# Attention scores split between GpSimd and VectorE: half of the squares of 16, a later row sum and an earlier fold

## The chip, the cores and the metric

The kernel runs on one core of a Trainium2 chip, as one program. The metric is the device time of one execution in microseconds (us). The engines are TensorE (PE in the profile; PEld is its weight load), VectorE (DVE), ScalarE (ACT), GpSimd (POOL) and SyncE (SP). POOL and SP issue the DMAs of this kernel.

## What is computed

A block of a small network over x of 8 batches x 512 tokens x 256 features, fp32: attention A, FFN, attention B, FFN again, each on the layer norm of x and added to it. The change touches attention A alone. It is an odd attention: for each token and each of its 16 heads, the 64 channels of Q attend to the 64 channels of K of the same token.

```python
Q = (x @ Wq + bq).reshape(b, s, H, C) * inv_sqrt_c      # H = 16, C = 64
K = (x @ Wk + bk).reshape(b, s, H, C)
V = (x @ Wv + bv).reshape(b, s, H, C)
scores = jnp.einsum('bshq,bshk->bshqk', Q, K)
mask = jnp.triu(jnp.ones((C, C), dtype=bool), 1)
scores = jnp.where(mask, -jnp.inf, scores)
w = jax.nn.softmax(scores, axis=-1)
attn = jnp.einsum('bshqk,bshk->bshq', w, V)
```

So every token and head has a 64 x 64 lower triangle of products q_i * k_j, their exponentials, and two row sums: of the exponentials, and of the exponentials times v_j. Nothing of this is a matmul; it is elementwise work on DVE, ACT and POOL.

## The kernel before

Tokens lie on the 128 partitions. A cell is one batch b (8), one group g of four heads (4) and one tile i of 128 tokens (4): 128 cells. The triangle of a cell is cut into the diagonal, and squares of 32, 16, 8, 4, 2 and 1 below it. They make four units (`units`, `NU`): unit 0 has the squares of 32 of two heads, unit 1 the squares of 16 of all four, unit 2 the squares of 32 of the other two heads, unit 3 all small squares. Each unit holds two halves in one tile, the exponentials e and the products e*v. Units 0 and 2 share the tag "w" with three buffers; unit 1 has the tag "w16" and unit 3 the tag "ws", with one buffer each.

A unit goes through these stages, each a method of `AttentionA`:

- `scores` (L765; the multiply is L784): q_i * k_j into the first half, two pieces of 128x1024 for the units 0 to 2. Before the change the units 0 and 2 are on POOL, which reads q from a copy in SBUF, and the units 1 and 3 on DVE.
- `exps` (L789; L798): exponential on ACT.
- `weigh` (L800; L808): e * v_j on DVE.
- `halve` (L810; L814): an accumulating DMA of 1 MB, issued by POOL, adds the second half of the columns of the tile to the first half (units 0 to 2).
- `fold` (L816; L819): for the units 0 and 2, POOL adds halves once more, 2048 columns to 1024.
- `gather` (L838; L845): row sums on DVE into small tiles `red`; the tile of the unit is free after it. The pairs (n, red) are put on the list `self.sums`.
- `add_rows` (L848; L852): POOL adds the sums to the cell's `acc`, which starts with the diagonal. `small_squares` (L828) does the same for the squares of 2 and 1, with L835.
- `invert` (L854; L856): reciprocal of the sum of exponentials on DVE; `divide` (L858; L860): the product on POOL.

Before `scores`, `project` computes q, k, v with PE, and `keep_qk` copies k and q to SBUF with ACT. After `divide`, `turn_group`, `project_out` and `new_x` bring the result back to x.

All engines but SP follow an order written out by hand: instructions stand on each engine in the order in which the Python program emits them. The order is `step(n)` (L638), a software pipeline over all 512 units: step n emits the scores of unit n, the weighing and halving DMA of unit n - 2, the fold of a unit n - 3 or n - 4, and so on. A step has three parts, split by `yield`. Between the parts the loop at the end of the file emits pieces of the generator `after_a` (FFN, attention B and FFN of batches whose attention A is done), at a rate set by `total`. So the first 75 steps have attention A alone with preparation, and the end has the last batch's FFN alone.

The generator `later_weights` (L411) prepares weights of the later stages on POOL, ACT and SP, and bounds on the inputs. `fit_qkv(g)` subtracts a row from the weights of head group g (group 0 on DVE, the others on POOL) and stores them to DRAM for later loads by `load_w` on SP. `measure(b)` (L726) makes mean and variance of x for the layer norm of a batch.

Of the kernel before, what the change touches and what calls it, by code (L numbers as in the profile page):

```python
# [9 lines left out]
F32 = mybir.dt.float32  # L10
# [3 lines left out]
ALU = mybir.AluOpType  # L14
AX = mybir.AxisListType

P = 128
# [9 lines left out]
GW = GH * C  # L27
NG = HID // GW
# [256 lines left out]
def fast_path(ctx: ExitStack, tc: tile.TileContext, k, t, flag):  # L285

    nc = tc.nc
# [8 lines left out]
    ap_ = ctx.enter_context(tc.tile_pool(name="ap", bufs=2))  # L296
# [257 lines left out]
    NU = len(units)  # L554
# [12 lines left out]
    def pieces(w, n, off, nsq, cols):  # L567

        def of_rows(v):
            return v[:, cols].rearrange("p (x t) -> p x t", t=2 * n)[:, :, n:]

        def of_cols(v):
            return v[:, cols].rearrange("p (x t) -> p x t", t=2 * n)[:, :, :n]

        if n < 16:
            e, ev = (  # L580
                w[:, a * SMALL + off : a * SMALL + off + nsq * n * n].rearrange("p (x i j) -> p x i j", i=n, j=n)
                for a in range(2)
            )
            yield e, ev, lambda v: of_rows(v).unsqueeze(3), lambda v: of_cols(v).unsqueeze(2)
            return
        both = w.rearrange("p (b a x i j) -> p a b x i j", a=2, x=nsq, i=n, j=JB)
        if n == 32:
            for x in range(nsq):
                yield (
                    both[:, 0, :, x],  # L590
                    both[:, 1, :, x],
                    lambda v, x=x: of_rows(v)[:, x].unsqueeze(1).unsqueeze(3),
                    lambda v, x=x: of_cols(v)[:, x].rearrange("p (b j) -> p b j", j=JB).unsqueeze(2),
                )
        else:
            for k in range(n // JB):
                yield (
                    both[:, 0, k],
                    both[:, 1, k],
                    lambda v: of_rows(v).unsqueeze(3),  # L600
                    lambda v, k=k: of_cols(v)[:, :, k * JB : (k + 1) * JB].unsqueeze(2),
                )

    class AttentionA:
# [32 lines left out]

        def step(self, n):  # L638

            weighed = self.at(n - 2)  # L640
            if weighed[0] is not None:
                self.weigh(*weighed)
            unit = self.at(n)
            on_pool = unit[3] in (0, 2)
            if on_pool:
                half = self.scores(*unit)
                next(half)
            if weighed[0] is not None:
                self.halve(*weighed)
            if on_pool:  # L650
                next(half, None)
            b, i, g, u = self.at(n + 40)
            if u == 0 and g == 0 and i == 0 and b > 0:
                self.x[b] = load_x(b)
            b, i, g, u = self.at(n + 10)
            if u == 0 and g == 0 and i == 0:
                self.measure(b)
            b, i, g, u = self.at(n + 8)
            if u == 0 and g == 0:
                self.live["xn"] = normed(self.x[b][:, i, :], *self.rn[b, i], "a")  # L660
            b, i, g, u = self.at(n - 5)
            if u == NU - 1:
                self.invert(b, i, g)
            b, i, g, u = self.at(n - 4)
            if u == 1:
                self.gather(b, i, g, u)
            b, i, g, u = self.at(n + 7)
            if u == 0 and g == 0:
                nc.scalar.copy(self.live[b, i], self.live.pop("ps_ln"))
            if self.at(n - 1)[0] is not None:  # L670
                self.exps(*self.at(n - 1))
            yield
            if unit[0] is not None and not on_pool:
                for _ in self.scores(*unit):
                    pass
            for args in self.sums:
                self.add_rows(*args)
            self.sums = []
            b, i, g, u = self.at(n - 5)
            if u == NU - 1:  # L680
                self.divide(b, i, g)
            b, i, g, u = self.at(n - 2)
            if u == NU - 1:
                self.small_squares(b, i, g)

            b, i, g, u = self.at(n - 4)
            if u == 0:
                self.fold(b, i, g, u)
            b, i, g, u = self.at(n - 3)
            if u == 2:  # L690
                self.fold(b, i, g, u)
            b, i, g, u = self.at(n - 9)
            if u == NU - 1:
                self.new_x(b, i, g)
            b, i, g, u = self.at(n + 2)
            if u == 0:
                self.keep_qk(b, i, g)
            b, i, g, u = self.at(n - 7)
            if u == NU - 1:
                self.turn_group(b, i, g)  # L700
            b, i, g, u = self.at(n - 8)
            if u == NU - 1:
                self.project_out(b, i, g)
            b, i, g, u = self.at(n + 3)
            if u == 0:
                self.project(b, i, g)
            yield
            b, i, g, u = self.at(n - 4)
            if u == 2:
                self.gather(b, i, g, u)  # L710
            b, i, g, u = self.at(n - 5)
            if u == 0:
                self.gather(b, i, g, u)
            b, i, g, u = self.at(n - 3)
            if u == NU - 1:
                self.gather(b, i, g, u)
            b, i, g, u = self.at(n - 7)
            if u == NU - 1:
                nc.scalar.copy(self.live["att"], self.live.pop("pta"))
            b, i, g, u = self.at(n + 8)  # L720
            if u == 0 and g == 0:
                self.live[b, i] = lnp.tile([P, DC, P], F32, tag="xnt_a", name=f"xnta_{b}_{i}", bufs=NT)
                self.live["ps_ln"] = turned_over(self.live.pop("xn"), half_bank().rearrange("p (c s) -> p c s", c=DC))
            yield
# [40 lines left out]
        def scores(self, b, i, g, n_u):  # L765

            qv, kt = self.live[b, i, g][:2]
            if n_u == 0:
                acc = ap_.tile([P, 2, GW], F32, tag="acc", name=f"acc_{b}_{i}_{g}", bufs=3)
                self.live[b, i, g].append(acc)  # L770
                nc.vector.tensor_tensor(acc[:, 0, :], qv[:, 0], kt[:, 0], ALU.mult)

            if n_u in (0, 2):
                w = wt.tile([P, 4096], F32, tag="w", name=f"w_{b}_{i}_{g}_{n_u}", bufs=3)
            elif n_u == 1:
                w = wt.tile([P, 4096], F32, tag="w16", name=f"w16_{b}_{i}_{g}")
            else:
                w = wt.tile([P, 2 * SMALL], F32, tag="ws", name=f"ws_{b}_{i}_{g}")
            self.live[b, i, g, n_u] = w
            eng, q = (nc.gpsimd, kt[:, 1]) if n_u in (0, 2) else (nc.vector, qv[:, 0])  # L780
            for n, off, nsq, cols in squares(units[n_u]):
                for e, ev, rows, columns in pieces(w, n, off, nsq, cols):
                    shape = list(e.shape)
                    eng.tensor_tensor(  # L784
                        e, rows(q).to_broadcast(shape), columns(kt[:, 0]).to_broadcast(shape), ALU.mult
                    )
                    yield
# [50 lines left out]
        def gather(self, b, i, g, n_u):  # L838


            w = self.live.pop((b, i, g, n_u))
            for n, off, nsq, cols in squares(units[n_u]):
                if n > 2:
                    red = ap_.tile([P, 2, nsq * n], F32, tag=f"red{nsq * n}", name=f"red_{b}_{i}_{g}_{n_u}_{n}", bufs=2 + (n < 32))
                    nc.vector.tensor_reduce(red, self.columns_of(w, n, off, nsq), AX.X, ALU.add)  # L845
                    self.sums.append((b, i, g, n, cols, red))

        def add_rows(self, b, i, g, n, cols, part):  # L848

# [491 lines left out]
    with tc.manual_schedule(engines={ET.PE, ET.DVE, ET.Activation, ET.Pool}):  # L1341
        a = AttentionA()
        prep = later_weights()
        fit_qkv(0)
        weights = None
        done, spent = after_a(), 0
        for n in range(-10, a.steps):
            for part, _ in enumerate(a.step(n)):
                if n >= 2:
                    next(prep, None)  # L1350
                while 3 * spent * each < total * (3 * (n - each - 11) + part + 1):
                    spent += next(done)
            if 0 <= n < NG - 1:
                fit_qkv(n + 1)
        for _ in done:
            pass
    judge()
# [86 lines left out]
```

## Time and profile before

| what | us |
|---|---|
| median of 3 runs | 4010.42 (4006.96 to 4017.54) |
| time of the profiled execution | 4009.55 |
| its span | 4007.6 |
| L784 on POOL (scores of 32), 512 | 1076.2 busy, 2102 ns each |
| L784 on DVE, 128x1024 of the squares of 16, 256 | 301.3 busy, 1219 ns each |
| L819 on POOL (fold), 256 | 643.1 busy, 2512 ns each |
| L814 on POOL (halving DMA issue), 384 | 337.1 busy, 878 ns each |
| L852 on POOL, row sums of 32 (128x128), 256 | 179.4 busy, 701 ns each |
| L852 on POOL, other row sums of a `red` (128x256), 384 | 291.6 busy, 759 ns each |
| L845 on DVE, row sums of 16 (128x256 out of 128x2048), 128 | 292.0 busy, 2281 ns each |
| L845 on DVE, row sums of 32 (128x128 out of 128x1024), 256 | 309.7 busy, 1210 ns each |
| L856 on DVE (reciprocal), 128 | 223.2 busy, 1744 ns each |

A line of the profile names the source line, the engine, the operation and the tiles (out<-in), the shape, a count, the busy time and the mean duration of one. In a timeline the first column is the start and the second the duration, both in us, and the bracket says how long the engine stood idle before the instruction and what ended that. Neighbours overlap a little on an engine, so the distance from start to start is shorter than the duration. Work of one engine lies beside that of the others, so busy times don't add up to the span.

### The profile page before, as it was taken

The numbers are of one execution on the slowest core, as the hardware profiler recorded it, in microseconds if no ns is written. First come the engines' busy times: TensorE is split into PE (matmuls) and PEld (weight loads), VectorE is DVE, ScalarE is ACT, GpSimd is POOL, SyncE is SP. The second block draws the span as 40 slices with busy tenths as digits, with TensorE's granted clock in tenths as the row PEclk, the third lists the DMA queues.
The fourth block names the chain that finished last, engine by engine and source line by source line (L and its number), as shares of the span: only waits on it lengthen the run. The fifth ranks groups of instructions, "written<-read, shape, count | busy, mean of one in ns | idle before, by whom it ended". The sixth has DMA issues, their size and how long they took to land.

```text
span 4007.6 us, 37678 instructions
## 1 busy us (share of the span) xinstructions
PE 2958.0 (74%) x12328; PEld 2012.2 (50%) x12328; DVE 3376.7 (84%) x3777; ACT 2337.2 (58%) x3145; POOL 3098.1 (77%) x3051
## 2 busy tenths in 40 slices
PE   1543478777876888768787788768787778768988
PEld 0311145355653656346553566346653556436847
DVE  4899988998889888998989988998889988897115
ACT  2433465666755766666755767567656667555342
POOL 6688888887888887887888888888888878886211
PEclk7555689888987989889897889879898899879999
DMA  8566777668776777668776688668877687767304
GB/s 240 114 141 145 146 182 182 147 161 199 199 162 126 195 188 196 150 147 210 174 192 139 168 198 214 147 131 198 195 181 151 154 199 205 155 133 210 126 29 167
DMA packets 118653, 671.07 MB, mean 167 GB/s; under 512 B 12704, under 2 KB 31915, under 8 KB 43824
## 3 DMA queue, kind: packets, MB, share of 16 engines
q0 software_dynamic: 78336, 570.46, 62.9%
q1 hardware_dynamic: 40112, 98.11, 6.8%
q8 instruction: 100, 1.64, 0.2%
q14 instruction: 105, 0.86, 0.1%
HBM read 255.90 MB, written 9.96 MB: 66 GB/s over the span
## 4 chain that ended last, share of the span: by engine, by line
DVE 38%; PE 16%; POOL 14%; DMA 12%; issue 8%; ACT 8%; POOLq 0%; DVEq 0%; ACTq 0%
DVE red L845 15%; DMA w<-w 12%; DVE w L808 10%; PE ph L1120 5%; ACT w L798 3%; POOL w L819 3%; DVE ws L808 3%; POOL w L784 3%; PE pqkb L1167 3%; DVE ws L784 3%; POOL acc L852 3%; DVE w L784 2%; POOL w L814 2%; DVE acc L856 2%; POOL h L1036 2%
## 5 line engine op out<-in xcount | busy, mean ns | idle before, releaser
L798 ACT ACTIVATE w<-w 128x2048 f32<-128x2048 f32 x384 | 734.2, 1913 | 653.8 <-POOL w L784 440.8
L1120 PE MATMUL ph<-h,hidden 128*128 128x512 f32 x4096 | 1047.9, 412 | 77.4 <-POOL h L1036 45.5
L784 POOL TENSOR_TENSOR w<-k 128x1024 f32<-128x1024 f32 x512 | 1076.2, 2102 | 9.6 <-ACT k L762 9.0
L1120 PEld LDWEIGHTS ph<-h,hidden 128*128 128x128 f32 x4096 | 795.3, 196 | 282.1 <-POOL h L1036 55.9
L808 DVE TENSOR_TENSOR w<-w,qv 128x1024 f32<-128x1024 f32 x768 | 899.8, 1213 | 22.4 <-ACT w L798 22.3
L845 DVE TENSOR_REDUCE red<-w 128x128 f32<-128x1024 f32 (+1 forms) x384 | 601.8, 1567 | 171.6 <-DMA w<-w 94.6
L819 POOL TENSOR_TENSOR w<-w 128x1024 f32<-128x1024 f32 x256 | 643.1, 2512 | 72.5 <-DMA w<-w 71.9
L814 POOL DMA_DIRECT2D w<-w x384 | 337.1, 878 | 339.7 <-issue 134.8
L852 POOL TENSOR_TENSOR acc<-acc,red 128x256 f32<-128x256 f32 (+1 forms) x640 | 471.0, 736 | 152.3 <-DVE red L845 124.5
L845 DVE TENSOR_REDUCE red<-ws 128x256 f32<-128x2048 f32 (+1 forms) x256 | 435.5, 1743 | 0.0
L746 PE MATMUL qv<-wqv,xnta 128*128 128x512 f32 x512 | 299.3, 715 | 89.9 <-DVE ws L808 82.4
L808 DVE TENSOR_TENSOR ws<-ws,qv 128x1024 f32<-128x1024 f32 (+3 forms) x512 | 294.7, 638 | 49.4 <-ACT ws L798 49.4
L1052 PE MATMUL pw<-xnt,gate 128*128 128x512 f32 (+2 forms) x1152 | 298.8, 419 | 24.9 <-ACT silu L1028 18.0
L784 DVE TENSOR_TENSOR w<-qv,k 128x1024 f32<-128x1024 f32 x256 | 301.3, 1219 | 3.6
L784 DVE TENSOR_TENSOR ws<-qv,k 128x1024 f32<-128x1024 f32 (+3 forms) x512 | 299.8, 648 | 0.0
L868 PE MATMUL bank<-ident,acc 128*128 128x128 f32 x256 | 64.3, 341 | 287.5 <-ACT k L761 287.1
L798 ACT ACTIVATE ws<-ws 128x1920 f32<-128x1920 f32 x128 | 231.5, 1809 | 75.3 <-DVE ws L784 74.7
L1052 PEld LDWEIGHTS pw<-xnt,gate 128*128 128x128 f32 x1152 | 227.6, 213 | 82.1 <-ACT silu L1028 22.3
L1229 ACT ACTIVATE eb<-psb 128x256 f32<-128x256 f32 (+3 forms) x512 | 182.2, 443 | 146.6 <-PE psb L1226 146.3
L1146 PE MATMUL pof<-w,h 128*128 128x256 f32 x1024 | 247.9, 396 | 19.4 <-ACT h L1085 19.4
L1085 ACT ACTIVATE h<-ph,s_sb 128x512 fp32r<-128x512 f32 (+1 forms) x256 | 171.1, 688 | 145.9 <-PE ph L1120 144.6
L856 DVE RECIPROCAL acc<-acc 128x256 f32<-128x256 f32 x128 | 223.2, 1744 | 12.3 <-POOL acc L852 12.3
(143 smaller groups left out, 4723.5 us busy)
## 6 DMA issues: line engine op xcount, KB each, us to landing
w<-w POOLq DMA_DIRECT2D x384, 1024.0 KB, 7.7
hidden<-in_h POOLq DMA_DIRECT2D x128, 1024.0 KB, 7.9
gate<-in_w12p POOLq DMA_DIRECT2D x32, 1024.0 KB, 9.0
w<-w_d SPq DMA_DIRECT2D x16, 1024.0 KB, 12.0
wqv<-wqv_d SPq DMA_DIRECT2D x31, 512.0 KB
wo<-in_wo SPq DMA_DIRECT2D x32, 256.0 KB, 7.4
wbqk<-wbqk_d SPq DMA_DIRECT2D x8, 1024.0 KB
w<-in_h SPq DMA_DIRECT2D x8, 1024.0 KB, 7.0
```

Source lines behind the costliest of these rows:

```text
L746: nc.tensor.matmul(qv.rearrange("p j f -> p (j f)"), xnt[:, c, :], wqv[:, c, :], start=(c == 0), stop=(c == DC - 1),)
L784: eng.tensor_tensor(e, rows(q).to_broadcast(shape), columns(kt[:, 0]).to_broadcast(shape), ALU.mult)
L798: nc.scalar.activation(e, e, AF.Exp, scale=C**-0.5)
L808: nc.vector.tensor_tensor(ev, e, columns(qv[:, 1]).to_broadcast(list(e.shape)), ALU.mult)
L814: nc.gpsimd.dma_start(w[:, :2048], w[:, 2048:], accum_op=ALU.add)
L819: nc.gpsimd.tensor_tensor(w[:, :1024], w[:, :1024], w[:, 1024:2048], ALU.add)
L845: nc.vector.tensor_reduce(red, self.columns_of(w, n, off, nsq), AX.X, ALU.add)
L852: nc.gpsimd.tensor_tensor(rows, rows, part.rearrange("p a (x i) -> p a x i", i=n), ALU.add)
L856: nc.vector.reciprocal(acc[:, 0, :], acc[:, 0, :])
L1052: nc.tensor.matmul(pj[:, toks], w[:, m % 4, j, c, :], xs[:, p, c, toks], start=(p == 0 and c == 0), stop=(p == 1 and c == DC - 1),)
L1120: nc.tensor.matmul(pss[j], w[:, j, c, :], h_in(p, c), start=(p == 0 and c == 0), stop=(p == 1 and c == MC - 1),)
L1146: nc.tensor.matmul(po, h(0, c)[:, i * P : (i + 1) * P], w3[:, c, :], start=(c == 0), stop=False)
```

## The change

1. In `scores`, the engine is chosen for each piece: all pieces of the squares of 32, and the first of the two pieces of the squares of 16, go to POOL; the second piece of 16 and the small squares to DVE.
2. `gather` for the units 0 and 2 writes into two halves of one tile, `red` of 32, and only the later of them puts it on the list: one `add_rows` of 128x256 instead of two of 128x128. The row sums of unit 2 come a step later (n - 5, not n - 4), those of unit 0 a step earlier (n - 4, not n - 5).
3. `fold` of unit 0 moves from step n - 4 to n - 3, ahead of the step's scores and halving DMA.
4. `invert` and `divide` come a step later (n - 6, not n - 5). `invert` and the `gather` of unit 1 move to the front of their step, in this order; `divide` comes behind the fold of unit 2.
5. At the start: `measure(0)` comes ahead of `fit_qkv(0)`, the fits of the other groups come at steps 4, 14 and 24 rather than 0, 1 and 2, and the preparation advances once a step from step 3, rather than three times a step from step 2.

```diff
         def step(self, n):
 
+            b, i, g, u = self.at(n - 6)
+            if u == NU - 1:
+                self.invert(b, i, g)
+            b, i, g, u = self.at(n - 4)
+            if u == 1:
+                self.gather(b, i, g, u)
             weighed = self.at(n - 2)
             if weighed[0] is not None:
                 self.weigh(*weighed)
+            b, i, g, u = self.at(n - 3)
+            if u == 0:
+                self.fold(b, i, g, u)
             unit = self.at(n)
...
             b, i, g, u = self.at(n + 10)
             if u == 0 and g == 0 and i == 0:
-                self.measure(b)
+                if b > 0:
+                    self.measure(b)
...
-            b, i, g, u = self.at(n - 5)
-            if u == NU - 1:
-                self.invert(b, i, g)
-            b, i, g, u = self.at(n - 4)
-            if u == 1:
-                self.gather(b, i, g, u)
...
             self.sums = []
-            b, i, g, u = self.at(n - 5)
-            if u == NU - 1:
-                self.divide(b, i, g)
             b, i, g, u = self.at(n - 2)
             if u == NU - 1:
                 self.small_squares(b, i, g)
 
-            b, i, g, u = self.at(n - 4)
-            if u == 0:
-                self.fold(b, i, g, u)
             b, i, g, u = self.at(n - 3)
             if u == 2:
                 self.fold(b, i, g, u)
+            b, i, g, u = self.at(n - 6)
+            if u == NU - 1:
+                self.divide(b, i, g)
...
             b, i, g, u = self.at(n - 4)
-            if u == 2:
+            if u == 0:
                 self.gather(b, i, g, u)
             b, i, g, u = self.at(n - 5)
-            if u == 0:
+            if u == 2:
                 self.gather(b, i, g, u)
...
-            eng, q = (nc.gpsimd, kt[:, 1]) if n_u in (0, 2) else (nc.vector, qv[:, 0])
             for n, off, nsq, cols in squares(units[n_u]):
-                for e, ev, rows, columns in pieces(w, n, off, nsq, cols):
+                for p, (e, ev, rows, columns) in enumerate(pieces(w, n, off, nsq, cols)):
+
+                    on_pool = n == 32 or n == 16 and p == 0
+                    eng, q = (nc.gpsimd, kt[:, 1]) if on_pool else (nc.vector, qv[:, 0])
...
                 if n > 2:
-                    red = ap_.tile([P, 2, nsq * n], F32, tag=f"red{nsq * n}", name=f"red_{b}_{i}_{g}_{n_u}_{n}", bufs=2 + (n < 32))
-                    nc.vector.tensor_reduce(red, self.columns_of(w, n, off, nsq), AX.X, ALU.add)
-                    self.sums.append((b, i, g, n, cols, red))
+                    if n_u != 2:
+                        self.live["red", n] = ap_.tile(
+                            [P, 2, GW // 2], F32, tag=f"red{n // 32}", name=f"red{n}_{b}_{i}_{g}"
+                        )
+                    red = self.live["red", n]
+                    part = red[:, :, cols.start // 2 : cols.stop // 2]
+                    nc.vector.tensor_reduce(part, self.columns_of(w, n, off, nsq), AX.X, ALU.add)
+                    if n_u != 0:
+                        self.sums.append((b, i, g, n, slice(0, GW), red))
...
         prep = later_weights()
+        a.measure(0)
         fit_qkv(0)
         weights = None
         done, spent = after_a(), 0
         for n in range(-10, a.steps):
             for part, _ in enumerate(a.step(n)):
-                if n >= 2:
+                if n >= 3 and part == 2:
                     next(prep, None)
...
-            if 0 <= n < NG - 1:
-                fit_qkv(n + 1)
+            if n in (4, 14, 24):
+                fit_qkv(n // 10 + 1)
```

## The prediction

> **What bounds the kernel now.** I read the page's busy shares first, then a table of windows over a stretch where only attention A runs, then the timelines of GpSimd (POOL) and VectorE (DVE) in one period of that stretch, and last the view of the halving DMA's line.
>
> ```profile
> PE 2958.0 (74%) x12328; PEld 2012.2 (50%) x12328; DVE 3376.7 (84%) x3777; ACT 2337.2 (58%) x3145; POOL 3098.1 (77%) x3051
> ```
>
> No engine is full on average, so the stages must be looked at apart. A "cell" below is one (batch, token tile, head group): four steps, 128 cells in all. From 161 to 327 us seven cells run with little beside them:
>
> ```profile
> 208.00:232.00 24.00, 9.41 (x16) 4.49 (x16) 23.97 (x25) 9.12 (x9) 20.72 (x18) 0.57 0.79 176
> sum 166.00, PE 66.78 PEld 31.04 DVE 165.76 ACT 63.86 POOL 145.12; mean PE 9.54 PEld 4.43 DVE 23.68 ACT 9.12 POOL 20.73
> ```
>
> The columns after the width are PE, PEld, DVE, ACT, POOL. DVE is busy 165.76 of 166 us: here a cell lasts 23.7 us, exactly DVE's work, and POOL has 20.7 us of work. The POOL timeline of such a cell:
>
> ```profile
> 303.21 0.87 POOL L814 DMA_DIRECT2D w<-w  x1 [2.68 <-issue]
> 303.82 2.35 POOL L852 TENSOR_TENSOR acc<-acc,red 128x128 f32<-128x128 f32 x3
> 306.13 1.96 POOL L784 TENSOR_TENSOR w<-k 128x1024 f32<-128x1024 f32 x1
> 308.02 0.86 POOL L814 DMA_DIRECT2D w<-w  x1
> 308.63 2.24 POOL L784 TENSOR_TENSOR w<-k 128x1024 f32<-128x1024 f32 x1
> 310.55 1.00 POOL L860 TENSOR_TENSOR acc<-acc 128x256 f32<-128x256 f32 x1
> 311.24 2.63 POOL L819 TENSOR_TENSOR w<-w 128x1024 f32<-128x1024 f32 x1
> 313.73 0.81 POOL L852 TENSOR_TENSOR acc<-acc,red 128x256 f32<-128x256 f32 x1
> 314.42 0.69 POOL L835 TENSOR_TENSOR ws<-ws 128x256 f32<-128x256 f32 x1
> 315.19 1.66 POOL L852 TENSOR_TENSOR acc<-acc,ws 128x256 f32<-128x256 f32 x2
> 316.80 2.36 POOL L819 TENSOR_TENSOR w<-w 128x1024 f32<-128x1024 f32 x1
> 319.12 1.96 POOL L784 TENSOR_TENSOR w<-k 128x1024 f32<-128x1024 f32 x1
> 321.02 0.87 POOL L814 DMA_DIRECT2D w<-w  x1
> ```
>
> POOL stands still once per cell, 2.7 us, at the halving DMA of unit 1, which waits for DVE. Both folds (L819) come at least two steps, or some 9 us of other POOL work, after their own halving DMA. The slots (start to next start) are what I sum with: score piece 1.92, DMA issue 0.62, fold 2.33, row-sum add 0.69, L835 0.69, divide 0.69. DVE in the same cell:
>
> ```profile
> 307.45 1.74 DVE L856 RECIPROCAL acc<-acc 128x256 f32<-128x256 f32 x1
> 309.11 2.28 DVE L808 TENSOR_TENSOR ws<-ws,qv 128x1024 f32<-128x1024 f32 x4
> 311.31 2.28 DVE L845 TENSOR_REDUCE red<-w 128x256 f32<-128x2048 f32 x1
> 313.62 2.36 DVE L784 TENSOR_TENSOR w<-qv,k 128x1024 f32<-128x1024 f32 x2
> ```
>
> Reciprocal 1.66 to the next start, row sums of the squares of 16 2.31, and right behind them the next cell's scores of 16, both pieces on DVE. From the line of the halving DMA:
>
> ```profile
> DMA to landing us min/median/max: 6.9/7.7/16.7
> ```
>
> So no halving DMA ends less than 6.9 us after its issue starts.
>
> Later cells carry the FFN and attention B as well. From the starts of L784 on POOL, the 127 cells from 28.0 to 3641.4 us last 23.4 to 47.3 us, mean 28.45.
>
> **What the skill says.** "DMA: Bandwidth & Descriptors", section "Rules for kernel authors", says to issue a DMA early, compute, and wait on its semaphore late. The trace agrees: both folds do so. Its section "Anatomy of one DMA" prices a DMA at about 2.0 us plus bytes over 436 GB/s, an estimate of 4.4 us for 1 MB; measured is 6.9, so I use 6.9 to 7.0. "GPSIMD Engine Reference", section 3.1, has an fp32 tensor_tensor at 1.96 times VectorE's time; here a score piece is 2.10 us on POOL (mean) against 1.22 on DVE, 1.7 times. "Trainium Architecture", section "Inside one NeuronCore": engines have own instruction streams and meet only at semaphores; an early wait on POOL holds all behind it.
>
> **The change, part by part.**
>
> 1. Piece 0 of the scores of 16 goes to POOL. DVE loses one of two L784 pieces, about 1.17 us a cell; POOL gains 1.92 us (no such shape was seen on POOL: same element count, so between DVE's 1.2 and the 2.3 of a fold; I take the 1.92 of its neighbours).
>
> 2. Row sums of the two units of 32 share one tile and one add: POOL loses one of two 128-wide adds, 0.65 us. POOL's own work in a bare cell is then 5 x 1.92 + 3 x 0.62 + 2 x 2.33 + 4 x 0.69 + 0.69 + 2 x 0.81 + 0.69 = 21.9 us, DVE's 22.5.
>
> 3. The fold of unit 0 moves from step n-4 to n-3, ahead of the step's scores and halving DMA. In the built order POOL now runs: score piece of unit 2, halving DMA of unit 0, second score piece of unit 2, and then at once the fold of unit 0. Between issue and fold lie 0.62 + 1.92 us, and whatever FFN work falls there. The DMA needs 7.0: POOL stands 4.5 us (gap A). Behind it wait the halving DMA of unit 1, two adds and the next scores. The old 2.7 us at that halving DMA is swallowed: DVE is done by then.
>
> 4. The scores of 16 have one buffer (tag w16). Before, DVE both read and refilled it, so order alone served. Now POOL's piece waits for DVE's row sums of the cell before; these stand on DVE right behind the reciprocal (moved to the same place); and the reciprocal waits for the merged add of 32, which is POOL's last instruction ahead of its piece. The chain POOL add, DVE reciprocal 1.66, DVE row sums 2.3, POOL piece, with two or three signals of about 0.05, cannot be shortened by running ahead: POOL stands 4.1 us (gap B).
>
> 5. The row sums themselves are moved but the same in number; divide and fold of unit 2 keep over 10 us behind what they need.
>
> 6. Start: statistics ahead of the weights' subtraction, fits of later groups at steps 4, 14, 24, preparation once a step. Before, DVE stood 24.7 us once (about 88 to 112) behind a load for the bounds; with a step between issue and use most of that goes, but the queue of SP brings new waits (loads of a later group stand ahead of the FFN's weights). I take a gain of 10, between -15 and +25.
>
> **The sum.** A bare cell: 21.9 + 4.5 + 4.1 = 30.5 us against 23.7. For all cells I went through the built order of POOL and summed slots: attention 128 x 21.8 = 2790, FFN, weights and normalisation about 370, together 3160. Gap A is 128 x 4.5 = 576, of which 158 is filled by FFN work that stands inside; gap B 128 x 4.1 = 525, 50 filled. 3160 + 418 + 475 = 4053, less the last cell's 23 = 4030 for what took 3613 before.
>
> To it come: 25 us until the first cell, 366 + 5 from the last one to the end (4007.6 - 3641.4, and the gaps in it), the start's gain given back by half (+10). That is 4436, a floor: every landing at its minimum, no producer late. In the trace before, landings beyond what the new order covers (7.0, 8.9 and 12.3 us for units 0, 1, 2) add to 77 + 87 + 57 = 221 us; with a longer period fewer collide, I take half, 110. POOL also stands for FFN producers: L934 for PE 88 us, L1036 for ACT 20, normalisation for DVE some 50, together about 155; a third to a half stays, 55. 4436 + 110 + 55 = 4601 us span, against 4007.6. The profiled execution's own time is 2 us above its span and 0.9 below the median, so 4600 as time.
>
> **Rivals.**
>
> - *One gap only* (say FFN work fills one, or the reciprocal is earlier than I read). Cell by cell the larger of the old period and the new POOL sum is 3741 with gap A alone, 3744 with B alone: 25 + 3741 + 371 + 10 + some 45 of collisions = 4190 us. For: FFN work does fill up to 7.8 us of A in some cells. Against: 45 to 50 bare cells have nothing to fill with. 0.12.
> - *Waits add up more*: all 221 of landings and all 155 of producers, and the piece of 16 at 2.3 us (+50): 4436 + 426 = 4860. For: loads of FFN weights share the DMA engines, up to 16.7 us to landing. Against: POOL alone sets the pace, the rest has time. 0.11.
> - *Not slower*: DVE stays the bound, and POOL meets both waits late enough. It decides where POOL does at least 4.5 us of other work between halving and fold, and the add of 32 is 4 us old when the piece of 16 comes up. Then 29 cells at DVE's 23.7 gain 1.2 each (35 us) and the start 20: 3955. For: DVE full in the bare cells. Against: the built order has nothing in either place. 0.04.
> - That the change doesn't do what it says: the built order shows all parts; no chance of its own.
>
> **How the numbers follow.** My case, both gaps open, has 0.73 and 4600, on its own 4440 to 4760. With half of the worse rival the range is 4350 to 4830; left out are the one-gap case, the faster one and the far tail. A measurement of this kernel tells about 0.3% from no change: faster 0.03, same 0.01, slower 0.96.
>
> **What would show it.** Right: bare cells of 30 to 31 us; the fold of unit 0 idle about 4.5 us until its DMA; the POOL piece of 16 idle about 4 us until DVE's row sums; DVE well under 80% busy; reciprocal waiting for POOL. Wrong: bare cells below 27 us, or DVE still full from 161 to 327 us; then a gap isn't there.

## The result and the profile after

| | before | changed |
|---|---|---|
| median of 4 runs, us | 4008.69 (4004.39 to 4017.54) | 4679.98 (4677.76 to 4681.43) |
| ratio | 1 | 1.167, 95% interval 1.165 to 1.169 |
| span of the profiled execution, us | 4007.6 | 4679.7 |
| first score piece on POOL starts, us | 28.0 | 24.1 |
| from there to that of the last cell, us | 3613.4 | 4275.6 |
| from there to the end, us | 366.2 | 379.9 |

The change makes the kernel 671 us slower. The busy shares of the changed kernel:

```profile
PE 3036.1 (65%) x12328; PEld 2034.9 (43%) x12328; DVE 3241.5 (69%) x3649; ACT 2343.4 (50%) x3145; POOL 3313.5 (71%) x3051
```

DVE lost 135 us of work and POOL gained 215, and both are now less full than either was. In the 127 cells from POOL's first score piece to that of the last cell, POOL was busy for 3007 us and stood for 606 before; with the change it is busy for 3223 us and stands for 1053. So two thirds of the added time is standing still. The table of windows over four bare cells, the early ones with little but attention A (columns: PE, PEld, DVE, ACT, POOL, each with its count, then the granted TensorE clock, the DMA share and GB/s):

```profile
287.00:318.00 31.00, 8.60 (x16) 3.94 (x16) 22.75 (x24) 9.11 (x9) 22.58 (x19) 0.56 0.50 101
sum 124.00, PE 35.39 PEld 16.41 DVE 94.55 ACT 39.28 POOL 89.70; mean PE 8.85 PEld 4.10 DVE 23.64 ACT 9.82 POOL 22.43
```

A bare cell lasts 31.0 us on average (30.9 in most), where it lasted 23.7. No engine is full. The granted clock does not explain that: it is 0.56 in this cell and was 0.57 in the one of before that the prediction shows, and PE is busy for under 9 of 31 us. POOL's timeline in one of them says where it stands:

```profile
303.08 0.87 POOL L817 DMA_DIRECT2D w<-w  x1
303.69 2.24 POOL L787 TENSOR_TENSOR w<-k 128x1024 f32<-128x1024 f32 x1
305.61 0.99 POOL L861 TENSOR_TENSOR acc<-acc,red 128x256 f32<-128x256 f32 x1
310.62 1.95 POOL L787 TENSOR_TENSOR w<-k 128x1024 f32<-128x1024 f32 x1 [4.01 <-DVE red L853]
312.53 0.73 POOL L861 TENSOR_TENSOR acc<-acc,red 128x256 f32<-128x256 f32 x1
...
318.53 1.97 POOL L787 TENSOR_TENSOR w<-k 128x1024 f32<-128x1024 f32 x1
320.43 0.85 POOL L817 DMA_DIRECT2D w<-w  x1
321.03 2.23 POOL L787 TENSOR_TENSOR w<-k 128x1024 f32<-128x1024 f32 x1
328.09 2.34 POOL L822 TENSOR_TENSOR w<-w 128x1024 f32<-128x1024 f32 x1 [4.82 <-DVE acc L772]
330.37 0.87 POOL L817 DMA_DIRECT2D w<-w  x1
```

L787 is the score multiply, L817 the halving DMA, L822 the fold, L853 the row sums, L861 their add. Gap B is the 4.01 us ahead of the piece of 16 at 310.62, gap A the 4.82 us ahead of the fold at 328.09. The name behind gap A (L772 on DVE) is misleading: it ended 20 ns ahead of the fold, but the halving DMA issued at 320.43 landed at 328.02, and over the whole trace the view of L822 names the DMA. This landing took 7.60 us, with a load of SP (0.26 MB) under way beside it; in nine of the thirteen cells from the sixth on (177 to 582 us) gap A is 4.1 to 4.2 us. DVE beside it:

```profile
306.64 1.75 DVE L865 RECIPROCAL acc<-acc 128x256 f32<-128x256 f32 x1 [6.51 <-POOL acc L861]
308.31 2.23 DVE L853 TENSOR_REDUCE red<-w 128x256 f32<-128x2048 f32 x1
310.45 2.33 DVE L811 TENSOR_TENSOR ws<-ws,qv 128x1024 f32<-128x1024 f32 x4
```

DVE itself stands 6.51 us until POOL's add of 305.61 is done at 306.60; then come 1.67 us of reciprocal and 2.23 of row sums, and POOL's piece starts at 310.62. Each engine waits in turn for the other. In the list of waits of the whole execution:

```profile
DVE acc L865 <- POOL acc L861: 708.3, 121, 10.6
...
POOL w L787 <- DVE red L853: 476.4, 127, 5.3
POOL w L822 <- DMA w<-w: 473.4, 121, 8.0
```

(us in total, times, longest.) POOL has both waits in nearly every one of the 128 cells.

### The profile page after: what moved, and what is told of

Read it like the earlier page. It is cut to its first block, busy times and chain, and to the rows that moved or that the text cites. A ratio compares the mean times of both kernels' runs of the same rounds, so it can differ in the third digit from the quotient of the medians.

```text
span 4679.7 us, 38174 instructions
## 1 busy us (share of the span) xinstructions
PE 3036.1 (65%) x12328; PEld 2034.9 (43%) x12328; DVE 3241.5 (69%) x3649; ACT 2343.4 (50%) x3145; POOL 3313.5 (71%) x3051
## 4 chain that ended last, share of the span: by engine, by line
POOL 49%; issue 19%; DVE 15%; PE 11%; ACT 3%; DMA 2%; POOLq 0%; SPq 0%; DVEq 0%; ACTq 0%
POOL w L787 20%; POOL w L822 9%; DVE red L853 8%; POOL acc L861 7%; POOL w L817 5%; PE ph L1129 4%; DVE ws L811 2%; DMA w<-w 2%; DVE w L811 2%; POOL h L1045 2%; POOL acc L869 1%; PE pof L1155 1%; PE qv L747 1%; PE pw L1061 1%; PE pyb L1243 1%
## 5 line engine op out<-in xcount | busy, mean ns | idle before, releaser
L787 POOL TENSOR_TENSOR w<-k 128x1024 f32<-128x1024 f32 x640 | 1325.6, 2071 | 493.7 <-DVE red L853 476.4
L747 PE MATMUL qv<-wqv,xnta 128*128 128x512 f32 x512 | 443.5, 1017 | 1049.9 <-DVE ws L811 925.2
L822 POOL TENSOR_TENSOR w<-w 128x1024 f32<-128x1024 f32 x256 | 608.4, 2376 | 497.3 <-DMA w<-w 473.4
L853 DVE TENSOR_REDUCE red<-w 128x128 f32<-128x1024 f32 (+1 forms) x384 | 595.6, 1551 | 135.7 <-POOL w L822 122.0
L747 PEld LDWEIGHTS qv<-wqv,xnta 128*128 128x128 f32 x512 | 141.1, 303 | 1225.4 <-issue 727.5
L861 POOL TENSOR_TENSOR acc<-acc,red 128x256 f32<-128x256 f32 x512 | 440.9, 861 | 20.1 <-DVE red L853 10.0
L853 DVE TENSOR_REDUCE red<-ws 128x256 f32<-128x2048 f32 (+1 forms) x256 | 435.3, 1742 | 0.0
L817 POOL DMA_DIRECT2D w<-w x384 | 337.1, 878 | 24.1 <-DVE acc L772 15.2
L787 DVE TENSOR_TENSOR ws<-qv,k 128x1024 f32<-128x1024 f32 (+3 forms) x512 | 299.8, 648 | 0.0
L1155 PE MATMUL pof<-w,h 128*128 128x256 f32 x1024 | 237.3, 386 | 0.0
L1155 PEld LDWEIGHTS pof<-w,h 128*128 128x128 f32 x1024 | 200.1, 196 | 40.4 <-issue 13.0
```

The source lines that it names most:

```text
L747: nc.tensor.matmul(qv.rearrange("p j f -> p (j f)"), xnt[:, c, :], wqv[:, c, :], start=(c == 0), stop=(c == DC - 1),)
L787: eng.tensor_tensor(e, rows(q).to_broadcast(shape), columns(kt[:, 0]).to_broadcast(shape), ALU.mult)
L817: nc.gpsimd.dma_start(w[:, :2048], w[:, 2048:], accum_op=ALU.add)
L822: nc.gpsimd.tensor_tensor(w[:, :1024], w[:, :1024], w[:, 1024:2048], ALU.add)
L853: nc.vector.tensor_reduce(part, self.columns_of(w, n, off, nsq), AX.X, ALU.add)
L861: nc.gpsimd.tensor_tensor(rows, rows, part.rearrange("p a (x i) -> p a x i", i=n), ALU.add)
```

## The experiments

The length of a bare cell below is worked out from the starts of the first score piece on POOL (or of the reciprocals on DVE), as the mean over eight or more cells of the first 18 that carry nothing else; 31.0 us with the change, 23.7 before.

**One gap closed.** The changed kernel with the fold of unit 0 a step later, ahead of the merged add:

```diff
-            b, i, g, u = self.at(n - 3)
-            if u == 0:
-                self.fold(b, i, g, u)
             unit = self.at(n)
...
+            b, i, g, u = self.at(n - 4)
+            if u == 0:
+                self.fold(b, i, g, u)
             for args in self.sums:
                 self.add_rows(*args)
```

> The changed kernel with one move: the fold of unit 0 comes a step later, just ahead of the merged add of 32, so that 0.6 + 1.8 + 1.9 + 0.6 + 1.9 us and more of POOL work lie between its halving DMA and it. Two gaps (mine): gap A goes, gap B stays and grows to some 4.5 us, since the row sums of unit 0 now stand between fold and reciprocal; a bare cell 27 us against 30.9, the whole 4260 us (4190 to 4350). Rival, POOL simply has too much work: nothing is taken from it, so 4680 within 30. Rival, only gap B matters: over 4600.

Measured: 4548.71 us, ratio 1.134 (1.131 to 1.136); a bare cell 28.0 us. Gap A is gone from the timeline and gap B is at the expected 4.5:

```profile
315.65 2.61 POOL L822 TENSOR_TENSOR w<-w 128x1024 f32<-128x1024 f32 x1
317.95 0.98 POOL L861 TENSOR_TENSOR acc<-acc,red 128x256 f32<-128x256 f32 x1
323.40 1.95 POOL L787 TENSOR_TENSOR w<-k 128x1024 f32<-128x1024 f32 x1 [4.47 <-DVE red L853]
```

The bare cell came within 1 us of what was expected, but the whole missed its range by 200 us. What the list of waits shows for it: DVE now waits for that fold in all 128 cells.

```profile
DVE red L853 <- POOL w L822: 715.0, 128, 11.3
```

The row sums of unit 0 stand on DVE right behind the fold, so fold, row sums, reciprocal and row sums of 16 became one chain over two engines, and in the cells with FFN work DVE's FFN instructions lie in that chain too, as an FFN product (L1040) at 2011.46 us between the row sums and the reciprocal (mean of the cells 18 to 125: 33.2 us, against 34.0 with the change and 28.7 before). Too much POOL work cannot be the whole cause: the work is the same and 131 us are gone.

Next, the reciprocal and the row sums of 16 swapped on DVE, nothing else:

```diff
-            b, i, g, u = self.at(n - 6)
-            if u == NU - 1:
-                self.invert(b, i, g)
             b, i, g, u = self.at(n - 4)
             if u == 1:
                 self.gather(b, i, g, u)
+            b, i, g, u = self.at(n - 6)
+            if u == NU - 1:
+                self.invert(b, i, g)
```

> The changed kernel with two lines swapped: the row sums of the squares of 16 stand on DVE ahead of the reciprocal, and no longer wait for POOL's merged add. Two gaps (mine): gap B shrinks from 4.1 to about 1.9 us (the landing of unit 1's halving DMA at 7.0 us and 2.2 us of row sums, against POOL's turn at about 7.5 us after its issue), gap A stays; a bare cell 28.7 us, the whole 4400 us (4340 to 4470). Rival, too much POOL work: 4680 within 30. Rival, the one buffer of unit 1 is no matter: 4680 too.

Measured: 4516.22 us, ratio 1.126 (1.123 to 1.128), 46 us above the expected range; a bare cell 29.8 us. Gap B is 1.71 us, as expected (DVE's row sums of 16 now stand for their halving DMA, 430.4 us in the list of waits), and 1.09 us of standing for the weighing of unit 3, now behind the reciprocal, came in behind it:

```profile
303.45 1.95 POOL L787 TENSOR_TENSOR w<-k 128x1024 f32<-128x1024 f32 x1 [1.71 <-DVE red L853]
305.36 0.73 POOL L861 TENSOR_TENSOR acc<-acc,red 128x256 f32<-128x256 f32 x1
307.18 0.61 POOL L838 TENSOR_TENSOR ws<-ws 128x256 f32<-128x256 f32 x1 [1.09 <-DVE ws L811]
```

Two swapped lines are worth 164 us. Half of what the swap won in a bare cell was lost again to the next wait of the same in-order queue.

**Both gaps closed.** The swap, and fold and row sums of unit 0 at their old steps (`fold` at n - 4 behind the sums, `gather` at n - 5).

> The changed kernel with both gaps closed: fold and row sums of unit 0 at the steps they had before, and the row sums of 16 ahead of the reciprocal. All scores stay where the change put them. Two gaps (mine): POOL has 22.5 us of work in a bare cell and DVE 22.7, so 22.7 to 23.7 us a cell, the whole 3900 to 4050 us, about the kernel before or a little under. Rival, too much POOL work: over 4300. Rival, a third wait (DVE for the fold of unit 0): bare cells of 26 us and more, over 4200.

Measured: 4240.28 us, ratio 1.056 (1.055 to 1.058); a bare cell 26.0 us. Neither gap is left in the bare cells looked at, 440 us are gone, and yet the forecast of parity missed. The size is that of the rival with a third wait, though the wait is another one. DVE stands at the row sums of 16:

```profile
304.90 2.29 DVE L853 TENSOR_REDUCE red<-w 128x256 f32<-128x2048 f32 x1 [3.84 <-POOL acc L861]
307.11 1.74 DVE L865 RECIPROCAL acc<-acc 128x256 f32<-128x256 f32 x1
```

Again the named releaser only ended about the same time. The halving DMA of unit 1 that these sums need was issued at 295.63 and landed at 304.78: 9.2 us. That of unit 0, issued 3.8 us earlier, was still under way and landed at 299.30. The list of waits of this run:

```profile
DVE red L853 <- DMA w<-w: 404.7, 92, 11.7
```

So the third wait is a landing. With the reciprocal first it had been hidden behind the wait for POOL's add: in the changed kernel DVE's row sums stand 13.6 us in all for these DMAs.

**Single parts in the kernel before.** First the early fold alone:

```diff
             weighed = self.at(n - 2)
             if weighed[0] is not None:
                 self.weigh(*weighed)
+            b, i, g, u = self.at(n - 3)
+            if u == 0:
+                self.fold(b, i, g, u)
```

(and the old place taken out).

> The kernel before with the early fold of unit 0 alone (ahead of the scores and halving DMA of step n-3). Gap A as mine: POOL's 20.7 us and 4.5 us of standing, 25.3 us in a bare cell against 23.7, the whole 4080 to 4230 us. Rival, the gap only costs together with the moved scores: POOL has 3 us of idle time in a bare cell here, so 4010 to 4060.

Measured: 4218.55 us, ratio 1.051 (1.049 to 1.054); a bare cell 26.4 us. The view of the fold's line has `DMA w<-w: 474.8, 145` as what its engine stood for, where it was 71.9 in the kernel before. Gap A needs no help from the moved scores. POOL's 3 us of idle time in a bare cell did not absorb it: the cell is 2.7 us longer, 1.1 more than expected, and in the cell looked at POOL stands 1.75 us more for row sums of DVE.

Then the first piece of the scores of 16 on POOL alone:

```diff
+                for p, (e, ev, rows, columns) in enumerate(pieces(w, n, off, nsq, cols)):
+                    on_pool = n == 32 or n == 16 and p == 0
+                    eng, q = (nc.gpsimd, kt[:, 1]) if on_pool else (nc.vector, qv[:, 0])
```

> The kernel before with part 1 of the change alone: the first piece of the scores of 16 on POOL, no order changed. Two gaps (mine): the row sums of 16 end about 1 us after POOL's turn, so gap B is 1 us; POOL 20.7 + 1.9 + 1.0 against DVE's 22.7: bare cells of 23 to 24 us, the whole 3970 to 4070 us. Rival, too much POOL work: the piece costs 1.9 us in each of 128 cells, 4250 us.

Measured: 4167.19 us, ratio 1.038 (1.037 to 1.040); a bare cell 25.2 us. This is above the expected range and below the rival's 4250. The expected wait for the row sums of 16 is not there in the bare cell looked at (over the whole run it is 145.0 us, in 55 cells); another one is. POOL and DVE in one cell:

```profile
304.69 2.10 POOL L785 TENSOR_TENSOR w<-k 128x1024 f32<-128x1024 f32 x1
...
309.74 2.34 POOL L820 TENSOR_TENSOR w<-w 128x1024 f32<-128x1024 f32 x1
...
319.45 0.87 POOL L815 DMA_DIRECT2D w<-w  x1 [2.28 <-DVE w L809]
```

```profile
312.11 1.22 DVE L846 TENSOR_REDUCE red<-w 128x128 f32<-128x1024 f32 x1 [2.52 <-POOL w L820]
313.24 3.40 DVE L846 TENSOR_REDUCE red<-ws 128x256 f32<-128x2048 f32 x2
316.56 2.34 DVE L809 TENSOR_TENSOR w<-w,qv 128x1024 f32<-128x1024 f32 x2
```

The piece of 16 (304.69) pushes the fold of unit 2 (309.74) back; DVE's row sums of unit 2 wait for it (DVE's row sums stand 263.3 us for folds over the whole run), behind them stand the row sums of unit 3 and the weighing of unit 1, and for this POOL's next halving DMA waits. The piece lies on a loop through both engines, and its 1.9 us show nearly whole (1.5 us a bare cell), though neither engine is full. The later row sums of unit 2 in the change could break this loop; no run has them as the only addition to the moved scores, so that is not shown.

The edits of the start alone:

> The kernel before with the edits of the start alone (statistics ahead of the fit, fits at steps 4, 14 and 24, preparation once a step). My estimate: 10 us faster, between 15 slower and 25 faster. Rival, SP's order of loads makes the start slower: 4020 and more.

Measured: 3994.04 us, ratio 0.9955 (0.9938 to 0.9971). It is the only part tried alone that gains: 17.6 us, within the stated bounds. DVE no longer stands the 24.7 us behind the load for the bounds; its longest wait in the first 165 us is now 9.9 us.

**What gap B hangs on.** The changed kernel with all scores of 16 on DVE again (`on_pool = n == 32`):

> The changed kernel with the scores of 16 on DVE again (part 1 undone), its order kept. My chain: halving DMA of unit 0, 7 us, fold, POOL up to the merged add of 32, reciprocal, row sums of 16, weighing of unit 3, scores of 16, weighing and halving of unit 0: 28 us in a bare cell though POOL has only 20.6 us of work and no piece of its own to wait for; the whole 4350 to 4480 us. Rival, the POOL piece and its one buffer are what costs: bare cells of 25 us (POOL and gap A), the whole 4100 to 4250. Rival, POOL's work: 1.9 us a cell less than the change, 4430, with no DVE wait for the reciprocal.

Measured: 4627.48 us, ratio 1.153 (1.151 to 1.156); a bare cell 30.4 us. All three expectations missed. POOL's timeline:

```profile
305.78 0.98 POOL L861 TENSOR_TENSOR acc<-acc,red 128x256 f32<-128x256 f32 x1
310.84 0.73 POOL L861 TENSOR_TENSOR acc<-acc,red 128x256 f32<-128x256 f32 x1 [4.08 <-DVE red L853]
312.89 0.61 POOL L838 TENSOR_TENSOR ws<-ws 128x256 f32<-128x256 f32 x1 [1.32 <-DVE ws L811]
```

With the piece gone from POOL, gap B is unchanged at 4.08 us: the next in line, the add of the squares of 16, needs the same row sums. Then it stands 1.32 us more for the weighing of unit 3, which DVE does behind both. The one buffer of unit 1 is therefore not what opens the gap. Reciprocal ahead of row sums, with POOL's add in front of both, is; my chain of 28 us had left out that POOL's own adds wait for it.

Last of these, the change without its parts 1 and 3 (scores on DVE, fold and row sums of unit 0 at the old steps):

> The change without its first and third part: all scores of 16 on DVE, fold and row sums of unit 0 at the old steps; what stays is the merged late sum of 32, reciprocal and row sums of 16 at the front of their step, division later, and the start. Gap B as a chain (mine): DVE stands at the reciprocal for POOL's add of 32, some 2.9 us a cell on top of its 23.7, so bare cells of 26 to 27 us, the whole 4200 to 4330. Rival, gap B is the price of the moved scores alone: bare cells of 23.7, the whole 3980 to 4030.

Measured: 4312.00 us, ratio 1.075 (1.073 to 1.077); a bare cell 27.5 us. The whole lies in the expected range, the bare cell half a microsecond above its own; the rival that gap B is the price of the moved scores alone (3980 to 4030) falls. DVE stands at the reciprocal for POOL's add, 481.2 us in the whole list of waits, and the moved scores have no part in it:

```profile
304.75 1.75 DVE L865 RECIPROCAL acc<-acc 128x256 f32<-128x256 f32 x1 [3.76 <-POOL acc L861]
```

**Looking for a better order.** With the loops known: all scores and late sums of the change, fold and row sums of unit 0 at the old steps, row sums of 16 behind the weighing of unit 3, reciprocal behind the scores of 16.

> The changed kernel with all its scores and late sums, in an order that I derive from the loops: fold and row sums of unit 0 at the old steps, the row sums of 16 behind the weighing of unit 3, the reciprocal behind the second piece of 16. Waits as I count them: POOL 22.3 us of work and 0.3 us of standing in a bare cell, DVE 22.7: 22.6 to 23.4 us a cell, the whole 3900 to 4000 us, less than before. Rival, landings of the halving DMA of unit 1 (8 to 9 us behind that of unit 0) still bound it, as in the run with both undone: bare cells over 25 us, over 4150.

Measured: 4135.60 us, ratio 1.030 (1.029 to 1.032); most bare cells 24.3 us, with some of 25.4. It missed; the rival was right in kind, though its numbers were not reached: the halving DMA of unit 1 was issued at 316.21 and landed at 325.39. PE now waited 607.9 us for the division too. Two more moves against these two:

```diff
+            first = unit[3] == 2
+            if first and weighed[0] is not None:
+                self.halve(*weighed)
             if on_pool:
                 half = self.scores(*unit)
                 next(half)
-            if weighed[0] is not None:
+            if not first and weighed[0] is not None:
                 self.halve(*weighed)
```

(and `turn_group`, `project_out`, `new_x` a step later).

> The order of the run before it (old steps for fold and row sums of unit 0, row sums of 16 behind the weighing of unit 3, reciprocal behind the scores of 16), with two more moves: the halving DMA of unit 0 goes ahead of both score pieces of its step (issued 1.9 us sooner, so that of unit 1 is less behind it in the queue), and what follows the division (transposes on PE and the rest) comes a step later, since PE stood 608 us for the division there. If the queue of halving DMAs held the bare cells at 24.2 us and PE's wait the FFN cells: bare cells of 23 to 23.7 us, the whole 3930 to 4040 us. If the loops on DVE and POOL hold it without the DMA: 24 us and more, 4080 to 4140.

Measured: 4098.92 us, ratio 1.022 (1.020 to 1.024); bare cells of 22.6 to 24.6 us, 23.4 on average. The bare cell is as expected and a little under the kernel before, but the whole isn't; it lies in the range of the other case. The cells 18 to 125, which carry FFN work, last 29.6 us on average, against 28.7 before. PE waits for ScalarE's copies there (354.5 us at L745); that this is what makes them longer is not shown, and what an order for those cells would have to look like stays open. No order tried here makes the moved scores pay; the best version of all is the kernel before with the edits of the start.

## Why the prediction was right

The forecast was 4600 us in a range of 4350 to 4830; measured were 4680. By its own steps:

| term of the sum | predicted, us | measured, us |
|---|---|---|
| until the first cell | 25 | 24.1 |
| POOL's work, 127 cells | 3137 | 3223 |
| gap A with late landings | 418 + 110 | 493 |
| gap B | 475 | 474 |
| other standing of POOL | 55 | 86 |
| start, part given back | 10 | in the rows above |
| last cell to the end | 371 | 380 |

- Part 3, gap A: forecast 4.5 us a bare cell, measured 4.1 to 4.2 in most and 4.82 in the one shown, whose DMA took 7.60 us; the run with the early fold alone shows it by itself. Shown.
- Part 4, gap B: forecast 4.1 us, measured 4.01, 476.4 us in all (the last 3 of them behind the 127 cells of the table). The chain (add, reciprocal, row sums) is shown by the swap and by the run with the scores back on DVE. The place that the step gave to the one buffer "w16" was too large: without a POOL piece in it the gap stays, taken by the next add.
- Parts 1 and 2, POOL's work: the mis-sized term. 21.9 us in a bare cell were forecast; 22.7 are left of most bare cells' 30.9 when the two gaps are taken off. The adds of 8 and 4, one behind the other on the same `acc`, take 1.77 us to the next start and not twice 0.69; the three adds at 303.82 us of the trace before, 2.35 us together, already said so. And the sum took slots from start to start, though an instruction that stands ahead of a gap shows its whole duration: 0.99 and not 0.69 us for the add ahead of gap B, 2.23 and not 1.92 for the piece ahead of gap A (which makes gap A that much shorter). The whole term is 86 us over. The other terms (-1, -35, -1, +31, -10, +9) nearly cancel, so the miss of 79 is about this term; that they cancel is luck.
- A reading that was wrong without consequence: of the two folds before, only that of unit 0 came two steps behind its DMA. That of unit 2 came one step, 8.8 us, behind (308.02 to 316.80 us).
- Part 1's gain on DVE is there (135 us less work) and worth nothing, since DVE no longer sets the pace: 94.55 of 124 us busy in the four cells.
- Part 6, the start: forecast 10 us of gain, measured 17.6 alone; in the changed kernel the first four cells last 120.0 us and not 135.8.
- The rival of one gap only (4190) falls: both are in nearly every cell. The worse one (4860) took all landings and producers; other standing came to 86 us instead of 155. The faster one needed other work inside the gaps, and there is none in bare cells.

Alone, the early fold costs 207 us, the moved scores 154, the late sums with the reciprocal's new place 319 (the run without parts 1 and 3, its gain at the start taken off), and the start gives back 18: 662 together, against 671 measured. None of these runs has the earlier row sums of unit 0. That the parts add up this closely was not expected and is not explained; undone from the other end, one gap gives 131 and the other 164, and both 440.

## What to carry to other kernels

Where engines run fixed orders, an edit has to be followed round the loop: for each instruction that is moved, ask what it waits for, what stands behind it on its engine, and which of those the other engine needs to come back. Busy shares of 84 and 77% did not tell what could be added here: in the kernel before, a wait that was placed 2.5 us behind a DMA of 7 us made a bare cell 2.7 us longer, although POOL had 3 us idle. Before giving work to a second engine, look whether the piece lies on such a loop: 1.9 us of work cost 1.5 us a bare cell although the engine had 3 us idle.

## What the runs showed of the hardware

Accumulating DMAs of 1 MB from the same queue land 5.1 to 5.2 us apart when they are issued 2.8 to 4.6 us apart (320.33 and 325.39; 322.52 and 327.67; 325.15 and 330.35 us in three runs), where one with no other of them under way mostly lands 6.9 to 7.0 us after its issue (7.6 in the cell of gap A above). So the second of these close pairs took 7.5 to 9.2 us, and issuing the first one further ahead of it (4.6 rather than 2.8 us) took the second from 9.2 to 7.5 us. From 160 to 520 us of each of the twelve traces, the later of two times, 6.94 us after the issue and 5.15 us after the landing before, meets the landings with a median error under 0.1 us; in eleven of the twelve a tenth of them came about 0.5 us or more later than that.
